# A convolution and GRU kernel: the first x chunks and cond turned by TensorE from whole rows, and three of the first chunk's four blocks convolved on 32x32 diagonal tiles

## The chip, the cores and the metric

The kernel runs on one core of one Trainium2 chip. The metric is the device time in microseconds (us) of one execution.

## The reference

The input x has 16 batch rows, 256 time steps and 512 channels, cond has 16 rows of 512 channels, all in float32. First, a causal convolution over time adds to x, channel by channel; its 16 taps are the 16 rows of cond. Then a GRU with hidden state of 512 runs over the 256 steps, starts from cond as its state, and its states are added:

```python
y = conv_general_dilated(x, cond[:, None, :], window_strides=(1,), padding=[(15, 0)],
                         feature_group_count=512)   # depthwise, causal, 16 taps
x = x + y
def cell(h, x_t):
    i_r, i_z, i_n = split(x_t @ W_ih + b_ih, 3)
    h_r, h_z, h_n = split(h @ W_hh + b_hh, 3)
    r, z = sigmoid(i_r + h_r), sigmoid(i_z + h_z)
    n = tanh(i_n + r * h_n)
    return (1 - z) * n + z * h
return x + scan(cell, cond, x)
```

## The kernel before

Channels lie on the 128 partitions, in four blocks (q = 0 to 3) along the free dimension. Partition 32 j + l of block q holds channel 128 j + 32 q + l. Time is cut into 16 chunks of 16 steps (`CHUNKS`); one block of a chunk has 16 steps x 16 batch rows = 256 columns. `xT` holds a chunk of x in this layout, with a halo of 15 steps in front, and `x1T` the convolved chunk x + conv.

The kernel writes out the order of every engine by hand: instructions run on each engine in the order in which the code issues them, and semaphores make one engine wait for another. SP's queue, ACT's queue and POOL's queue issue the transfers. The 16 steps' work of a later chunk is dealt out over the GRU's steps by `Plan`, from costs and due times; the first piece of it, `bulk.run(0, HEAD)`, is issued ahead of step 0.

What stands ahead of the GRU:

- cond (four transfers of 128 channels) and chunks 0 and 1 of x (`load_x`, L125, eight transfers each, in pieces of 512 bytes, on the SP, ACT and POOL queues) come in with 32 partitions for each j, so that a transposition of 32x32 squares by DVE gives the layout: `prepare_cond` (L192) and `turn_units` (L222).
- `load_weights` (L173) then issues W_ih and W_hh, each gate in four slices of 32 partitions, on SP and POOL. A queue reuses its semaphores in turn, so that some issues wait for the landing of an earlier transfer.
- `mark` and `idle_products(PAD)` (L350, L356) issue filler products on PE at the start; PAD is 108.
- Chunk 0 is convolved by two engines. For blocks 0 and 1, DVE does a first product with cond's last tap plus one (L554), then 15 taps each (L265), shorter and shorter. For blocks 2 and 3 (`Q_PE`), `conv_on_tensor` lets ACT make 16 diagonal matrices of 128x128 for each block (L288), and PE multiplies each by a shifted view of `xT` and adds up in PSUM (L292). ACT evicts the two results (L300).
- For chunk 1, ACT does the first products of the four blocks (`first_terms`, L239) and DVE the 15 taps of each. A tap waits for the first product of its block.
- PE then does the biases (`spread_biases`, L362), the input products of the n gate for the first 8 steps (`ni_units`, L320, evicted by ACT at L332) and those of r and z for the first two steps (`pair_units`, L383).

One GRU step (`step`) on PE is: products of r, of n, of z (L418), then some of the input products for later steps. DVE looks at r (`seen`, L398, so that DVE's wait for ACT stands there), multiplies r and h_n (L447), transposes (L449), adds (L451), transposes z (L461), and scans (L474) for the new state, which the next step's products on PE wait for. DVE's taps of the next chunk stand in the same order between the steps: in step 0, before the look at r.

Of the kernel before, what the change touches and what calls it, by code (L numbers as in the profile page):

```python
# [24 lines left out]
F32 = mybir.dt.float32  # L25
BF16 = mybir.dt.bfloat16
AF = mybir.ActivationFunctionType
ALU = mybir.AluOpType
PSUM = bass.MemoryType.PSUM

P = 128
L = 32
GT = 8
R, Z, N = 0, 1, 2
CHUNKS = (16,) * 16
PAD = 108
HEAD = 11.0
SYNC = mybir.DependencyInfo(mybir.DependencyClass.Sync, mybir.DependencyReason.DATA)
Q_PE = (2, 3)
NI = 8  # L40
AHEAD = 10
ROOM = 2.05
# [33 lines left out]
def conv_gru_kernel(  # L76
# [10 lines left out]
    nc = tc.nc  # L87
    B, T, C = x.shape
    K = cond.shape[0]
    NQ = C // P  # L90
    assert B == 16 and K == B and NQ == 4 and sum(CHUNKS) == T
    HALO = (K - 1) * B
# [5 lines left out]
    starts = [sum(CHUNKS[:c]) for c in range(NCH)]  # L98

    const = ctx.enter_context(tc.tile_pool(name="const", bufs=1))  # L100
# [5 lines left out]
    op = ctx.enter_context(tc.tile_pool(name="op", bufs=3))  # L106
    dram = ctx.enter_context(tc.tile_pool(name="dram", bufs=1, space=bass.MemoryType.DRAM))
    ps = ctx.enter_context(tc.tile_pool(name="ps", bufs=1, space=PSUM))
    ps_ni = ctx.enter_context(tc.tile_pool(name="ps_ni", bufs=2, space=PSUM))

    ctx.enter_context(tc.manual_schedule())

    def by_part(natural):
        return natural.rearrange("p (q l) -> p q l", q=NQ)
# [4 lines left out]
    def load_x(c, queues=((nc.sync,), (nc.sync,)), behind=None):  # L119

        n = CHUNKS[c]
        t = xin.tile([P, max(CHUNKS) // 2, P], F32, tag="x_nat", name=f"x_nat_{c}")
        for s in range(2):
            for j in range(NQ):
                made = queues[s][j % len(queues[s])].dma_start(  # L125
                    out=t[32 * j + B * s : 32 * j + B * s + B, 0 : n // 2],
                    in_=x[:, starts[c] + s : starts[c] + n : 2, j * P : (j + 1) * P],
                )
                if s == j == 0 and behind is not None:
                    tc.add_manual_dep(made.ins, behind.ins.name, SYNC, reason="later in time")  # L130
        x_nat[c] = t

    cond_nat = const.tile([P, P], F32)
    nc.vector.memset(cond_nat, 0.0)

    warm = const.tile([P, 1], F32)
    nc.vector.memset(warm, 0.0)
    blank = const.tile([P, 2 * P], BF16)
    nc.vector.memset(blank, 0.0)
    for j in range(NQ):  # L140
        (nc.sync, nc.scalar)[j % 2].dma_start(
            out=cond_nat[32 * j : 32 * j + B, :], in_=cond[:, j * P : (j + 1) * P]
        )
    load_x(0, ((nc.sync, nc.scalar), (nc.gpsimd,)))
    nc.scalar.activation(warm, warm, AF.Sigmoid)
    ident = const.tile([P, P], F32)
    make_identity(nc, ident)


    b_two = const.tile([2, 3 * C], F32)  # L150
# [3 lines left out]
    bn_nat = const.tile([P, P], F32)  # L154
    nc.vector.memset(bn_nat, 0.0)

    load_x(1, ((nc.sync,), (nc.gpsimd,)))
    nc.sync.dma_start(out=b_two[0:1, :], in_=b_hh.rearrange("(o c) -> o c", o=1))
    nc.sync.dma_start(
        out=b_two[1:2, 0 : 2 * C], in_=b_ih[0 : 2 * C].rearrange("(o c) -> o c", o=1)  # L160
    )
    nc.gpsimd.dma_start(
        out=bn_nat[0:P:L, :], in_=b_ih[2 * C : 3 * C].rearrange("(j c) -> j c", j=NQ)
    )


    wih_rz = const.tile([P, NQ, 2 * C], F32)
    wih_n = const.tile([P, NQ, C], F32)
    whh = [const.tile([P, NQ, C], F32, name=f"whh_{g}") for g in range(3)]

    def load_weights(w_sb, w, g, queues):
        for j in (0, 2, 1, 3):
            queues[j].dma_start(  # L173
                out=w_sb[L * j : L * j + L],
                in_=w[j * P : (j + 1) * P, g * C : g * C + w_sb.shape[2]].rearrange(
                    "(q l) c -> l q c", l=L
                ),
            )


    for tile_of, g in ((wih_n, N), (wih_rz, R)):
        load_weights(tile_of, w_ih, g, (nc.sync, nc.sync, nc.gpsimd, nc.gpsimd))
    zero_z = [const.tile([P, NQ * B * 2], F32, name=f"zero_z_{i}") for i in range(2)]
    for t in zero_z:
        nc.gpsimd.memset(t, 0.0)


    condT = const.tile([P, NQ, L], F32)
    last1 = const.tile([P, NQ], F32)

    def prepare_cond():
        nc.vector.transpose(condT, by_part(cond_nat))  # L192
        nc.vector.tensor_scalar_add(last1, condT[:, :, K - 1], 1.0)

    bnT = const.tile([P, NQ, L], F32)

# [3 lines left out]
    xT, x1T, ni = {}, {}, {}  # L200
# [3 lines left out]
    evictions = []  # L204
# [7 lines left out]
    def turn_units(c):  # L212

        def halo():
            xT[c] = xtp.tile([P, NQ, HALO + CMAX], F32, tag="xT", name=f"xT_{c}")
            if c:
                m = CHUNKS[c - 1] * B
                nc.scalar.copy(xT[c][:, :, 0:HALO], xT[c - 1][:, :, m : m + HALO])

        def turn(a):  # L220
            o = HALO + a * PAIR
            nc.vector.transpose(  # L222
                xT[c][:, :, o : o + GT * B].rearrange("p q (a r) -> p a q r", r=L),
                x_nat[c][:, a : a + GP].rearrange("p a (q l) -> p a q l", q=NQ),
            )
            if 2 * (a + GP) == CHUNKS[c] and 4 < c + 3 < NCH:
                load_x(c + 3)

        return [(0.0, halo)] + [
            (0.7, lambda a=a: turn(a)) for a in range(0, CHUNKS[c] // 2, GP)  # L230
        ]

    def first_terms(c):

        x1T[c] = x1p.tile([P, NQ, CMAX], F32, tag="x1T", name=f"x1T_{c}")
        n = CHUNKS[c] * B

        def first(q):
            nc.scalar.activation(  # L239
                x1T[c][:, q, 0:n],  # L240
                xT[c][:, q, HALO : HALO + n],
                AF.Copy,
                scale=last1[:, q : q + 1],
            )

        for q in range(NQ):
            firsts.append((c, q, lambda q=q: first(q)))

    def give_firsts(most=99):
        for _ in range(min(most, len(firsts))):  # L250
            firsts.pop(0)[2]()

    def lag(k):

        return (K - 1 - k) * B
# [19 lines left out]
            (0.135 + n / 960.0, lambda k=k, q=q: tap(k, q)) for k in range(K - 1) for q in range(NQ)  # L275
        ]

    def conv_on_tensor():

        n = CHUNKS[0] * B  # L280
        diag = const.tile([P, len(Q_PE), K, P], F32)

        def weight(k, q):
            return condT[:, q, k : k + 1] if k < K - 1 else last1[:, q : q + 1]

        for i, q in enumerate(Q_PE):
            for k in reversed(range(K)):
                nc.scalar.activation(diag[:, i, k], ident, AF.Copy, scale=weight(k, q))  # L288
        for i, q in enumerate(Q_PE):
            acc = ps_ni.tile([P, CHUNKS[0] * B], F32, tag="pni", name=f"conv_{q}")  # L290
            for k in reversed(range(K)):
                nc.tensor.matmul(  # L292
                    acc[:, lag(k) : n],
                    lhsT=diag[:, i, k],
                    rhs=xT[0][:, q, HALO : k * B + n],
                    start=(k == K - 1),
                    stop=(k == 0),
                    skip_group_check=True,
                )
            evictions.append(lambda q=q, acc=acc: nc.scalar.copy(x1T[0][:, q, 0:n], acc[:, 0:n]))  # L300


    blocks = [(t0, NI) for t0 in range(0, T, NI)]
# [43 lines left out]
    def mark():  # L347

        for i in range(2):
            nc.tensor.matmul(rz[i], lhsT=blank[:, 0:P], rhs=blank, start=True, stop=True)  # L350
            nc.tensor.matmul(nh[i], lhsT=blank[:, 0:P], rhs=blank[:, 0:P], start=True, stop=True)

    def idle_products(n):

        for _ in range(n):
            nc.tensor.matmul(  # L356
                spare[0:L, 0, 0:1], lhsT=blank[:, 0:L], rhs=blank[:, 0:1], start=True, stop=True
            )
# [180 lines left out]
    bulk = Plan()  # L539
    mark()  # L540
    idle_products(PAD)
    nc.tensor.drain()
    (_, halo), *turns = turn_units(0)
    halo()
    for t in hist:
        nc.vector.memset(t[:, 0:L], 0.0)
    prepare_cond()
    for _, fn in turns:
        fn()
    first_terms(0)  # L550
    firsts.clear()
    for q in range(NQ):
        if q not in Q_PE:
            nc.vector.tensor_scalar_mul(  # L554
# [1 line left out]
                xT[0][:, q, HALO : HALO + CHUNKS[0] * B],  # L556
                last1[:, q : q + 1],
            )
    conv_on_tensor()

    taps = [fn for i, (_, fn) in reversed(list(enumerate(tap_units(0)))) if i % NQ not in Q_PE]
    needed = (NI - 1) * (NQ - len(Q_PE))
    for fn in taps[:needed]:
        fn()
    for _, fn in turn_units(1):
        fn()
    nc.vector.transpose(bnT, by_part(bn_nat))
    for fn in taps[needed:]:
        fn()
    evictions.pop(0)()  # L570
    first_terms(1)
    give_firsts()
    evictions.pop(0)()
    spread_biases()
    nc.scalar.copy(b_rows, spare)
    seed_rz(0)
# [14 lines left out]
    for c in range(1, NCH):  # L591
        due = starts[c] - NI
        taps = tap_units(c)
# [4 lines left out]
        at = len(taps) - AHEAD  # L598
# [1 line left out]
            bulk.add(cost, due, fn)  # L600
    bulk.run(0, HEAD)

    h = (lambda kc: condT[:, kc, 0:B], condT[:, :, 0:B])
    late = []
    of_pair, of_block = [], []
    for t in range(T):
        p, s = divmod(t, 2)
# [23 lines left out]
        h = step(t, h, bulk_work, other_products)  # L631
# [41 lines left out]
```

## Time and profile before

| | |
|---|---|
| median of 3 runs | 1041.6 us (1041.51 to 1042.34) |
| profiled execution: span of the core, first to last instruction | 1039.8 us |
| distance of the span to the median | 1.8 us |
| PE busy | 1022.6 us, 98% |
| DVE busy | 926.8 us, 89% |
| ACT busy | 380.3 us, 37% |
| POOL busy | 12.4 us, 1% |
| HBM read and written | 14.73 MB and 8.39 MB |

The profiled execution has no time of its own beside its span in the page; the span leaves out what lies ahead of the first instruction and behind the last. Times in the views are us from the start of the span. In a timeline a row gives start, duration, engine, line, operation, output<-input and the count of instructions merged; in brackets stands the idle time before it and what ended it. In a table by stretch, each engine has its busy us and, in parentheses, its instructions. A matmul in float32 is recorded as two instructions. "PEld" is the loading of PE's stationary operand, which overlaps with its products.

### The profile page before, as it was taken

To read this page: it belongs to the slowest core of one execution; us is meant where nothing else is said; L and a number is where in the kernel's file an instruction comes from. 1 tells how busy PE (TensorE), PEld (TensorE's weight loads), DVE (VectorE), ACT (ScalarE), POOL (GpSimd) and SP (SyncE) were. 2 spreads that over 40 slices of the span, in tenths; PEclk is the share of its full clock that TensorE was granted. 3 is DMA by queue.
4 is the path that set the end of the run, shared out by engine and by line. 5 is a ranking of instruction groups with operands and counts; after the bars stand their busy time and mean duration, and the time that the engine had idled before them with its cause. 6 is when DMAs were issued, how large, how long until landed. Compare 5 with 4: busy or idle time off the path is not lost.

```text
span 1039.8 us, 71852 instructions
## 1 busy us (share of the span) xinstructions
PE 1022.6 (98%) x32952; PEld 928.5 (89%) x32952; DVE 926.8 (89%) x3606; ACT 380.3 (37%) x1520; POOL 12.4 (1%) x29
## 2 busy tenths in 40 slices
PE   7899999999999999999999999999999999999997
PEld 6699999999999999999999999999999999999986
DVE  7899999999999999999999999999999999896555
ACT  6233433334333333433334333343433334333332
POOL 4000000000000000000000000000000000000000
PEclk9999999999999999999999999999999999999999
DMA  9420101101010010100100010010000000000000
GB/s 216 111 58 13 26 15 29 21 15 31 8 35 14 15 35 8 32 15 19 30 14 26 14 34 15 15 34 5 15 14 15 15 13 6 15 15 15 14 11 17
DMA packets 40850, 27.72 MB, mean 27 GB/s; under 512 B 6686, under 2 KB 38498, under 8 KB 40548
## 3 DMA queue, kind: packets, MB, share of 16 engines
q1 hardware_dynamic: 38756, 18.78, 8.0%
q8 instruction: 257, 4.21, 1.7%
q0 software_dynamic: 1376, 4.20, 1.7%
q14 instruction: 45, 0.37, 0.1%
q10 hardware_dynamic: 416, 0.16, 0.1%
HBM read 14.73 MB, written 8.39 MB: 22 GB/s over the span
## 4 chain that ended last, share of the span: by engine, by line
PE 95%; DMA 3%; DVE 1%; SPq 0%; issue 0%; ACT 0%; DVEq 0%; ACTq 0%
PE prz L418 42%; PE pnh L418 21%; PE prz L383 20%; PE pni L320 10%; DMA whh<-in_L_cond_W_hh_dram 2%; DMA x_nat<-in_x_dram 1%; DVE rnT L449 0%; DVE zp L461 0%; DVE rn L447 0%; SPq L125 0%; ACT zero_z L465 0%; DVE n L451 0%; DMA out_dram<-o 0%; DVE hist L474 0%; DVE glance L398 0%
## 5 line engine op out<-in xcount | busy, mean ns | idle before, releaser
L418 PE MATMUL prz<-whh,hist 128*32 128x128 f32 x16320 | 539.9, 273 | 3.0 <-DVE hist L474 2.1
L418 PEld LDWEIGHTS prz<-whh,hist 128*32 128x32 f32 x16320 | 450.0, 103 | 8.5 <-DVE hist L474 6.6
L265 DVE SCALAR_TENSOR_TENSOR x1T<-xT,condT,x1T 128x256 f32<-128x256 f32 (+2 forms) x930 | 377.4, 462 | 0.0
L418 PE MATMUL pnh<-whh,hist 128*32 128x128 f32 x8160 | 269.7, 273 | 0.0
L383 PE MATMUL prz<-wih_rz,x1T 128*32 128x256 f32 x4096 | 268.2, 379 | 0.1
L418 PEld LDWEIGHTS pnh<-whh,hist 128*32 128x32 f32 x8160 | 226.7, 104 | 0.0
L459 ACT ACTIVATE dn<-n 128x64 f32<-128x64 f32 x256 | 67.9, 265 | 325.9 <-DVE n L451 325.9
L383 PEld LDWEIGHTS prz<-wih_rz,x1T 128*32 128x32 f32 x4096 | 129.0, 110 | 43.7 <-issue 0.3
L320 PEld LDWEIGHTS pni<-x1T,wih_n 128*32 128x32 f32 x4096 | 122.8, 110 | 42.7 <-ACT x1T L300 0.6
L435 ACT ACTIVATE r<-prz 128x128 f32<-128x128 f32 x256 | 71.1, 278 | 238.6 <-PE prz L418 235.5
L320 PE MATMUL pni<-x1T,wih_n 128*32 128x128 f32 x4096 | 158.1, 273 | 0.0
L474 DVE TENSOR_TENSOR_SCAN hist<-zero_z,dn 128x32 f32<-128x32 f32 (+1 forms) x768 | 128.6, 216 | 0.0
L447 DVE TENSOR_TENSOR rn<-r,pnh 128x128 f32<-128x128 f32 x256 | 72.4, 283 | 38.5 <-PE pnh L418 37.2
L465 ACT ACTIVATE zero_z<-zp 128x32 f32<-128x32 f32 x512 | 90.6, 226 | 8.6 <-DVE zp L461 1.8
L449 DVE STREAM_TRANSPOSE rnT<-rn 128x128 f32<-128x128 f32 x256 | 79.7, 311 | 8.7
L461 DVE STREAM_TRANSPOSE zp<-prz 128x128 f32<-128x128 f32 x256 | 80.9, 316 | 1.8 <-PE prz L418 1.7
L332 ACT ACTIVATE ni<-pni,bnT 128x128 f32<-128x128 f32 x128 | 47.1, 368 | 74.7 <-PE pni L320 74.7
L467 DVE TENSOR_TENSOR dn<-hist,dn 128x64 f32<-128x64 f32 x255 | 58.4, 229 | 11.3
L451 DVE TENSOR_TENSOR n<-rnT,ni 128x64 f32<-128x64 f32 x256 | 57.7, 225 | 8.9
L398 DVE COPY glance<-r 1x1 f32<-1x1 f32 x256 | 34.0, 133 | 25.3 <-ACT r L435 25.3
L371 ACT COPY prz<-b_rows 128x256 f32<-128x256 f32 x128 | 48.5, 379 | 0.0
L398 DVE COPY glance<-zero_z 1x1 f32<-1x1 f32 x256 | 36.3, 142 | 8.0 <-ACT zero_z L465 0.3
(51 smaller groups left out, 211.1 us busy)
## 6 DMA issues: line engine op xcount, KB each, us to landing
out_dram<-o SPq DMA_DIRECT2D x248, 32.0 KB, 1.7
x_nat<-in_x_dram SPq DMA_DIRECT2D x118, 64.0 KB, 3.0
whh<-in_L_cond_W_hh_dram POOLq DMA_DIRECT2D x8, 256.0 KB, 14.7
wih_rz<-in_L_cond_W_ih_dram POOLq DMA_DIRECT2D x2, 512.0 KB, 10.2
wih_rz<-in_L_cond_W_ih_dram SPq DMA_DIRECT2D x2, 512.0 KB, 14.3
whh<-in_L_cond_W_hh_dram SPq DMA_DIRECT2D x4, 256.0 KB, 19.0
x_nat<-in_x_dram POOLq DMA_DIRECT2D x8, 64.0 KB, 5.4
wih_n<-in_L_cond_W_ih_dram POOLq DMA_DIRECT2D x2, 256.0 KB, 7.7
```

The source lines that it names most:

```text
L265: nc.vector.scalar_tensor_tensor(out=x1T[c][:, q, to], in0=xT[c][:, q, k * B + to.start : k * B + n], scalar=condT[:, q, k : k + 1], in1=x ...
L320: nc.tensor.matmul(hold[q][32 * j : 32 * j + 32, 0:n], lhsT=wih_n[:, kc, j * P + q * L : j * P + q * L + L], rhs=x1T[c][:, kc, o : o + n], ...
L383: nc.tensor.matmul(rz[p % 2][32 * j : 32 * j + 32], lhsT=x1T[c][:, kc, o : o + PAIR], rhs=w_rz[:, :, j * P : (j + 1) * P], start=False, st ...
L398: nc.vector.tensor_copy(glances[i][0:1], of_scalar[0:1, 0:1])
L418: product = nc.tensor.matmul(dst[32 * j : 32 * j + m], lhsT=h[0](kc), rhs=whh[g][:, kc, j * P : (j + 1) * P], start=False, stop=(kc == NQ ...
L435: of_r = nc.scalar.activation(r, pr, AF.Sigmoid)
L447: nc.vector.tensor_mul(rn, r, pnh)
L449: nc.vector.transpose(rnT, by_part(rn))
L459: nc.scalar.activation(dn_v[:, :, :, 1], n, AF.Tanh)
L461: nc.vector.transpose(zp, by_part(pz))
L465: nc.scalar.activation(z_v[:, qs, :, 1], zp[:, qs, half], AF.Sigmoid) for qs in halves
L474: nc.vector.tensor_tensor_scan(hist_g[:, lo + at : lo + end], z[:, to], dn[:, to], 0.0, op0=ALU.mult, op1=ALU.add,)
```

## The change

`load_rows` replaces `load_x` for chunks 0 and 1: four transfers of 128 whole rows of x (half a chunk each, 2 KB a row), two on SP's queue and two on ACT's, none on POOL's. cond comes as one transfer of 16 rows on ACT's queue. `turn_by_tensor` multiplies 32-column slices of these rows by the identity on PE, 16 products for each tile, into one PSUM buffer (`turning`); DVE copies cond and chunk 0 out of it, ACT copies chunk 1.

`Q_PE` gets block 1 too, so DVE keeps block 0 alone. A diagonal matrix is no longer 128x128: `make_diag` makes for each block the four 32x32 diagonals of all 16 taps in one tile, with one product over 15 taps and one for the last (block 1 on DVE, blocks 2 and 3 on POOL, none on ACT). `conv_on_tensor` issues four products for each tap, each on 32 rows and 32 columns of PE, into one accumulator. Between the three convolutions PE turns the two halves of chunk 1. W_ih's issues now stand behind the diagonals in POOL's order, and so does the transfer of b_ih's n part. PAD is 72 and the drain behind the filler products is gone. The evictions of the three convolutions on ACT, all three, now stand ahead of chunk 1's first products.

```diff
-PAD = 108
+PAD = 72
-Q_PE = (2, 3)
+Q_PE = (1, 2, 3)
...
+    turning = ctx.enter_context(tc.tile_pool(name="turning", bufs=1, space=PSUM))
...
-    cond_nat = const.tile([P, P], F32)
-    nc.vector.memset(cond_nat, 0.0)
+    def load_rows(c, half, queue):
+        t = const.tile([P, C], F32, name=f"x_rows_{c}_{half}")
+        t0 = starts[c] + half * GT
+        queue.dma_start(out=t, in_=x[:, t0 : t0 + GT, :].rearrange("b t c -> t b c"))
+        x_rows[c, half] = t
+    x_rows = {}
+    cond_nat = const.tile([B, C], F32)
...
-    for j in range(NQ):
-        (nc.sync, nc.scalar)[j % 2].dma_start(
-            out=cond_nat[32 * j : 32 * j + B, :], in_=cond[:, j * P : (j + 1) * P]
-        )
-    load_x(0, ((nc.sync, nc.scalar), (nc.gpsimd,)))
+    nc.scalar.dma_start(out=cond_nat, in_=cond)
+    for c in range(2):
+        for half in range(2):
+            load_rows(c, half, (nc.sync, nc.scalar)[half])
...
+    ident_l = const.tile([P, L], F32)
+    nc.vector.tensor_reduce(out=ident_l, in_=ident.rearrange("p (i l) -> p l i", l=L),
+                            op=ALU.add, axis=mybir.AxisListType.X)
...
-    load_x(1, ((nc.sync,), (nc.gpsimd,)))
...
+    def turn_by_tensor(turned, rows, unit):
+        for q in range(NQ):
+            for j in range(NQ):
+                at = j * P + q * L
+                nc.tensor.matmul(turned[L * j : L * j + L, q], lhsT=rows[:, at : at + L],
+                                 rhs=unit, start=q == 0, stop=q == NQ - 1,
+                                 skip_group_check=True)
     def prepare_cond():
-        nc.vector.transpose(condT, by_part(cond_nat))
+        turned = turning.tile([P, NQ, K], F32, tag="turned", name="cond_turned")
+        turn_by_tensor(turned, cond_nat, ident[0:B, 0:B])
+        nc.vector.tensor_copy(condT, turned)
         nc.vector.tensor_scalar_add(last1, condT[:, :, K - 1], 1.0)
+    def turn_rows(c, half, engine):
+        turned = turning.tile([P, NQ, P], F32, tag="turned", name=f"x_turned_{c}_{half}")
+        turn_by_tensor(turned, x_rows[c, half], ident)
+        to = xT[c][:, :, HALO + half * P : HALO + half * P + P]
+        ...  # copied by ACT or by DVE
...
+    def make_diag(engine, q):
+        diag[q] = const.tile([P, K, L], F32, name=f"diag_{q}")
+        parts = ((slice(0, K - 1), condT[:, q, 0 : K - 1]), (slice(K - 1, K), last1[:, q : q + 1]))
+        for to, w in parts:
+            n = to.stop - to.start
+            engine.tensor_tensor(out=diag[q][:, to], op=ALU.mult,
+                in0=ident_l.unsqueeze(1).broadcast_to([P, n, L]),
+                in1=w.unsqueeze(2).broadcast_to([P, n, L]))
...
-        for i, q in enumerate(Q_PE):
-            for k in reversed(range(K)):
-                nc.scalar.activation(diag[:, i, k], ident, AF.Copy, scale=weight(k, q))
...
-                nc.tensor.matmul(acc[:, lag(k) : n], lhsT=diag[:, i, k],
-                    rhs=xT[0][:, q, HALO : k * B + n], ...
+            for j in range(NQ):
+                rows = slice(L * j, L * j + L)
+                nc.tensor.matmul(acc[rows, lag(k) : n], lhsT=diag[q][rows, k],
+                    rhs=xT[0][rows, q, HALO : k * B + n], ...
...
-    nc.tensor.drain()
...
     prepare_cond()
-    for _, fn in turns:
-        fn()
+    make_diag(nc.vector, Q_PE[0])
+    for q in Q_PE[1:]:
+        make_diag(nc.gpsimd, q)
+    nc.gpsimd.dma_start(out=bn_nat[0:P:L, :], ...)
+    for tile_of, g in ((wih_n, N), (wih_rz, R)):
+        load_weights(tile_of, w_ih, g, (nc.sync, nc.sync, nc.gpsimd, nc.gpsimd))
+    turn_units(0)[0][1]()
+    turn_rows(0, 0, nc.vector)
+    turn_rows(0, 1, nc.vector)
     first_terms(0)
...
-    conv_on_tensor()
+    conv_on_tensor(Q_PE[0])
+    turn_units(1)[0][1]()
+    turn_rows(1, 0, nc.scalar)
+    for q in Q_PE[1:]:
+        if len(evictions) > 1:
+            evictions.pop(0)()
+        conv_on_tensor(q)
+        if q == Q_PE[1]:
+            turn_rows(1, 1, nc.scalar)
...
-    for fn in taps[:needed]:
-        fn()
-    for _, fn in turn_units(1):
+    for fn in taps:
         fn()
     nc.vector.transpose(bnT, by_part(bn_nat))
-    for fn in taps[needed:]:
-        fn()
-    evictions.pop(0)()
     first_terms(1)
+    while evictions:
+        evictions.pop(0)()
     give_firsts()
-    evictions.pop(0)()
     spread_biases()
```

## The prediction

> **What bounds the kernel now.** The page's chain that ended last came first: PE holds 95% of the span, DMA 3%. The table by stretch shows PE full from 40 us on. A change that touches only what stands before step 0 therefore moves the end by as much as it moves the moment from which PE never stops.
>
> ```profile
> PE 95%; DMA 3%; DVE 1%; SPq 0%; issue 0%; ACT 0%; DVEq 0%; ACTq 0%
> ```
> ```profile
> 20.00:25.00 5.00, 5.00 (x142) 4.03 (x141) 5.00 (x14) 2.77 (x8) 0.55 (x1) 1.00 1.03 268
> ...
> 40.00:50.00 10.00, 10.00 (x344) 8.96 (x336) 9.66 (x38) 4.16 (x16) 0.00 (x0) 1.00 0.30 83
> ```
>
> (After the stretch: its length, then busy us of PE, PEld, DVE, ACT, POOL, the clock, the share of the DMA engines, GB/s.) The chain in order of time names that moment. The last W_hh slice lands at 34.07, its z products run, and from 36.33 PE goes on without a gap. I call 36.33 the restart.
>
> ```profile
> 11.42 22.65 DMA whh<-in_L_cond_W_hh_dram
> 34.07 0.14 issue
> 34.20 1.10 PE prz L418 x32
> ...
> 36.33 1.08 PE prz L418 x32
> ```
>
> So the start is bound by DMA, whose engines are full (share 1.03). The timeline of DVE shows how little lies behind that:
>
> ```profile
> 15.94 15.99 DVE L265 SCALAR_TENSOR_TENSOR x1T<-xT,condT,x1T 128x128 f32<-128x128 f32 x48
> 31.85 0.13 DVE L398 COPY glance<-r 1x1 f32<-1x1 f32 x1
> 32.78 0.29 DVE L447 TENSOR_TENSOR rn<-r,pnh 128x128 f32<-128x128 f32 x1 [0.80 <-PE pnh L418]
> ```
>
> The last 32 of these 48 are chunk 1's taps (28 of the head start, 4 of step 0); they start at 19.18, 0.396 us apart: 12.67 us. Step 0's look at r stands behind them in DVE's order. In step 1 PE starts again 1.85 us after that look (38.46 to 40.31, nothing else late). By DVE alone the restart would be 31.85 + 1.85 = 33.7: DVE has 2.6 us to spare, and what delays chunk 1's taps by more costs all beyond that.
>
> **What releases chunk 1's taps.** A tap needs ACT's first term of its block. In ACT's order before, the first terms follow the *first* convolution's eviction:
>
> ```profile
> 16.14 0.37 ACT L300 COPY x1T<-conv 128x256 f32<-128x256 f32 x1 [1.51 <-PE conv L292]
> 16.41 1.71 ACT L239 ACTIVATE x1T<-xT,last 128x256 f32<-128x256 f32 x4
> ```
>
> After, they follow all three evictions, because the loop that empties the list stands ahead of them. So chunk 1's taps wait for the end of the *third* convolution on PE. The rest is a sum of when that is.
>
> **Prices on PE.** Two rows of the products on 128x128 tiles, the same shapes (256 down to 176 columns) twice, show the clock, although the clock column says 1.00 for both:
>
> ```profile
> 9.36:13.52 4.16, 4.15 (x11) 3.76 (x12) 1.00 1.03 210
> 15.95:17.92 1.97, 1.97 (x12) 1.89 (x12) 1.00 1.03 292
> ```
>
> 4.16 us against 1.97: until 13.5 PE ran at half speed, after 4.2 us of unbroken products at full. The filler products (1.96 to 5.00) had not raised it. An f32 product is two instructions; on four column tiles, at full speed, 16 instructions of 256 columns take 0.86 us and 32 of 128 take 0.87, so 0.21 ns per column and instruction, four tiles at a time. No row shows four row tiles at once; the nearest are these.
>
> - A convolution after: 16 taps of 256 down to 16 columns (2,176 in all), each on four diagonal tiles: 2,176 x 4 x 2 x 0.21 = 3.7 us. The other end: nothing under 128 columns is cheaper than 128 (the filler's starts lie 26.7 ns apart however small): 4.4 us. I take 3.7, since the starts to four tiles lie 7 ns apart in the trace. At half speed 7.4.
> - Turning half a chunk of x: 16 products of 128 columns, 32 instructions: 0.87 us, at half speed 1.7.
> - The convolutions of before took 11.2 us for two blocks; three now take 11.1, one after another.
>
> On the four diagonal tiles the Trainium skill speaks against the change: "TensorEngine Tiling (Array Packing)", section Restrictions and Gotchas, says that different row tiles cannot access one PSUM bank at a time, and all four write one `acc`. Four times 3.7 would be 14.8 us a block and a time near 1080. But here each row tile writes partitions of its own, and the page does not say that the chip would wait, so I leave it to a rival.
>
> **The sum, in us from the start.**
> 1. The memset of cond_nat goes, so PE starts at 1.1; 72 fillers at 26.7 ns end at 3.75. cond is one transfer on ACT's queue, issued near 1.03; the 8 KB ones took 1.6 to 1.8 to land, so it is there. 16 small products at half speed, 0.5 to 0.9: take 0.7, and 0.2 to drain: 4.65. DVE's copy (64 columns, rows of 0.18 to 0.23): 4.9.
> 2. x, first half: its buffer is cond's, so PE starts at 4.95. The rows (issued at 1.0 to 1.9, 2 KB packets where 512 B were) should land by 4.5 to 5.5; 64 KB in 512 B pieces took 4.9. 1.7 at half speed and a drain: 6.85. DVE meanwhile makes block 1's diagonals (480 columns at the taps' 1.04 ns and 0.13: 0.63, plus 0.16 for last). Copy of 512 columns by the same: 0.66, 7.5. Second half, one buffer, so after that copy: 7.55 to 9.45; copy 10.1. Before, both transposes were through at 9.2.
> 3. First convolution: 3.5 us at half speed until 13.6 does 1.75 of its 3.7; the rest ends at 15.5.
> 4. x of chunk 1, first half, behind it in PE's order: 16.4. Second convolution: 20.1. Second half: 21.0. The third convolution's accumulator is the first's, and ACT evicts that only after both its copies of x: drain 0.2, copy 0.6 (rows: 384 columns 0.48, 960 columns 0.98), eviction 0.35: PE stands 1.1, to 22.1. Third convolution: 25.8.
> 5. Eviction and first term (0.37 and 0.43, starts 0.27 apart, drain and signals): 26.7. Taps: +12.67 = 39.4. Restart +1.85: 41.2, against 36.33: 4.9 later.
>
> Beside these, priced at nothing: DVE's single block of chunk 0 (a first product 0.3, 16 sizes at half of the 7.9 that two blocks took, 3.9) ends near 14.5, under PE's convolutions. On POOL the eight x issues (4.2 us) go; ahead of bn_nat and its W_ih and W_hh issues now stand four diagonal products that wait for last1 at 5.1. A 128-column select took 0.29; 480 columns cost 0.29 to 1.08 each: take 1.1 and 0.3 twice, so POOL issues from about 7.9 where bn_nat went at 6.13. The second convolution wants these diagonals at 16.4. bn_nat took 5.8 to land: 14, and DVE is idle then. SP loses eight issues (6 of them 2.78 us), so its weights, behind b_two's memset (near 3.6), start by 4.3 rather than 6.89. The bytes are the same, x's packets are four times fewer; W_hh should land between 29 and 36. A landing costs landing + 2.26 (34.07 to 36.33), so it decides only past 39. PE's biases (0.8), head products (3.85 and 1.2 of waits for ACT), pair (1.9) and step 0 (4.0) run from 25.8 to 37.6; zp is wanted at 39.4 + 0.9. DVE is last, alone.
>
> The sum goes on the median: 1041.6 + 4.9 = 1046.5. The page gives the profiled execution's span, 1039.8, 1.8 below the median; I keep that distance, so the span should be near 1044.7.
>
> **The rivals.**
> - *The clock rises early.* If filler, cond and x products (1.1 to 9.4 with two gaps under 1 us) raise it by about 6.8, the second half of x is 0.85 cheaper and the first convolution 1.75: restart 38.6, time 1043.9. For it: PE is busier there than before. Against: the filler did not raise it before. "TensorE: Matmul & The Clock Gate", Part 1, says that about 3.4 us of sustained activity is needed in a window that does not start with the kernel, so the phase decides; by the page alone either case could come.
> - *Short products at the 26.7 ns floor:* three times 0.7, 1048.6 with the late clock, 1046.0 with the early one.
> - *Row tiles one after another:* 3 x 11.1 more, near 1080.
> - *Faster: the queue's relief decides.* W_hh then lands near 30, and the restart falls to DVE. This needs the taps to start by 21.8 (36.33 - 1.85 - 12.67); with the early clock a convolution would have to cost 2.9 us. If they started at 19.2 as now, the restart would be 33.7 and the time 1039.0. Against it: 2.9 is a fifth under the column price that every four-tile row shows.
>
> **How the numbers follow.** 0.2%, about 2.1 us, is what a measurement here can tell from no change. Late clock, with either product price: 0.50 (1046.5 to 1048.6). Early clock: 0.36 (1043.0 to 1046.0, its lower end if x and cond are also half a us sooner); 0.15 of that lies under 1043.7. Serial tiles or another cost above 1052: 0.07. Faster: 0.07. The range 1042.8 to 1052 leaves out about 0.17. Faster 0.07, same 0.15, slower 0.78.
>
> **What would show it.** Right: in the timeline of DVE a hole of about 12 us between chunk 0's last tap and chunk 1's first, ended by ACT's first terms, which follow the eviction of the third convolution; glance of r near 39; W_hh landed before its products; convolutions of 3.7 us at full speed. Wrong: a first chunk 1 tap before 21.8; convolutions under 3 us or over 5; W_hh still last in the chain; a gap on PE after the restart.

## The result, and the profile after

The changed kernel takes 1059.5 us (median of 4 runs, 1058.2 to 1060.3), the kernel before beside it 1042.0: 1.016 times as long, 95% interval 1.014 to 1.018. The direction was right, and 1059.5 lies above the range (1042.8 to 1052.0). The profiled execution took 1059.2 us, with a span of 1057.4 where 1044.7 was forecast: 12.7 us too little.

The page's chain still belongs to PE; DVE's share is now 3% (1% before) and that of "issue" 1% (0% before):

```profile
PE 96%; DVE 3%; issue 1%; ACT 0%; DVEq 0%
```

The chain in order of time (start, us, what, and how many instructions of it) shows where the time lies. The restart is now 52.58 (36.33 before, 41.2 forecast):

```profile
17.71 1.14 PE conv L336 x17
18.85 2.12 issue
20.98 4.76 PE conv L336 x95
25.73 0.66 PE x_turned L206 x17
26.40 2.45 issue
28.85 1.11 PE x_turned L206 x15
...
30.99 6.22 PE conv L336 x126
...
38.05 12.77 DVE x1T L301 x32
...
52.58 1.93 PE prz L462 x32
54.51 1.69 PE pnh L462 x32
```

Three things are to be seen. Twice PE stops in the middle of a loop of products, for 2.12 and 2.45 us, with nothing that it waits for ("issue"); both times 17 instructions into a new tile. The third convolution takes 6.22 us, where 3.7 was priced. And after the restart 32 instructions of r take 1.93 and those of n 1.69, where such a group at full speed takes 0.87.

The timeline of DVE has the hole that was forecast, but 21 us of it and not 12. It is ended by ACT's first term, and then come the 32 taps and the look at r:

```profile
38.05 12.77 DVE L301 SCALAR_TENSOR_TENSOR x1T<-xT,condT,x1T 128x256 f32<-128x256 f32 x32 [21.07 <-ACT x1T L275]
50.73 0.14 DVE L442 COPY glance<-r 1x1 f32<-1x1 f32 x1
```

The table by stretch (after the stretch: length, busy us of PE, PEld, DVE, ACT, POOL, the clock, the share of the DMA engines, GB/s), cut where the clock changes, explains the slow products:

```profile
21.90:25.30 3.40, 3.40 (x75) 3.32 (x69) 0.00 (x0) 0.00 (x0) 0.83 (x2) 0.50 1.07 289
25.30:28.70 3.40, 1.10 (x49) 0.80 (x42) 0.00 (x0) 0.00 (x0) 0.55 (x1) 1.00 1.03 242
28.70:35.50 6.80, 5.59 (x67) 3.42 (x71) 0.00 (x0) 1.14 (x3) 0.00 (x0) 0.50 0.85 187
...
52.60:56.00 3.40, 3.40 (x66) 3.35 (x70) 2.32 (x8) 0.45 (x2) 0.00 (x0) 0.51 0.02 5
```

All edges of the clock lie on a grid of 3.41 us (15.09, 21.92, 25.33, 28.74, 35.57, 52.64, 56.05). The first stop lies in 18.5 to 21.9, the second in 25.3 to 28.7, the wait for the taps in 49.2 to 52.6: each time the next stretch runs at half speed. DMA is full (1.03 to 1.07) around both stops.

### The profile page after: what moved, and what is told of

Its sections match the earlier page's. It is cut to its first block, busy times and chain, and to the rows that moved or that the text cites. A ratio compares the mean times of both kernels' runs of the same rounds, so it can differ in the third digit from the quotient of the medians.

```text
span 1057.4 us, 72669 instructions
## 1 busy us (share of the span) xinstructions
PE 1036.2 (98%) x33396; PEld 933.9 (88%) x33396; DVE 924.5 (87%) x3590; ACT 372.7 (35%) x1491; POOL 11.0 (1%) x25
## 4 chain that ended last, share of the span: by engine, by line
PE 96%; DVE 3%; issue 1%; ACT 0%; DVEq 0%
PE prz L462 42%; PE pnh L462 21%; PE prz L427 20%; PE pni L364 10%; PE conv L336 2%; DVE x1T L301 1%; PE x_turned L206 1%; DVE rnT L493 0%; DVE rn L491 0%; DVE zp L505 0%; ACT zero_z L509 0%; DVE n L495 0%; PE spare L400 0%; DVE hist L518 0%; DVE xT L229 0%
## 5 line engine op out<-in xcount | busy, mean ns | idle before, releaser
L301 DVE SCALAR_TENSOR_TENSOR x1T<-xT,condT,x1T 128x256 f32<-128x256 f32 (+1 forms) x915 | 374.6, 464 | 21.6 <-ACT x1T L275 21.1
L427 PEld LDWEIGHTS prz<-wih_rz,x1T 128*32 128x32 f32 x4096 | 126.4, 110 | 45.1
```

Of the source, the lines that this page charges most:

```text
L301: nc.vector.scalar_tensor_tensor(out=x1T[c][:, q, to], in0=xT[c][:, q, k * B + to.start : k * B + n], scalar=condT[:, q, k : k + 1], in1=x ...
L427: nc.tensor.matmul(rz[p % 2][32 * j : 32 * j + 32], lhsT=x1T[c][:, kc, o : o + PAIR], rhs=w_rz[:, :, j * P : (j + 1) * P], start=False, st ...
```

## The theories

*Instruction fetch.* Between the weights' packets the trace has single packets of a queue that carries PE's instructions, 16,384 bytes each. The whole run has 261 of them for PE's 33,396 recorded matmuls, and the kernel before 257 for 32,952: one for every 128. The convolution on small tiles issues 128 of them per block where the 128x128 diagonals issue 32, and does so while the DMA engines are full. If the next packet comes late, PE stands at the end of what it has, and the stop lowers the clock for the next 3.4 us or more. Here is the table of the DMA queues between 18 and 21 us (packets, MB, share of 16 engines): the one packet ended at 19.34 (packet times are from the trace's own records), and PE went on at 20.98.

```profile
q0 software_dynamic: 139, 0.50, 67.2%
q1 hardware_dynamic: 110, 0.24, 32.0%
q8 instruction: 1, 0.02, 2.5%
```

The trace of before has one such stop, which the prediction passed over, because W_hh landed later anyway. In PE's timeline of before:

```profile
29.46 0.95 PE L418 MATMUL prz<-whh,condT 128*16 128x128 f32 x27 [1.14 <-issue]
```

It comes at PE's 346th recorded matmul, the first stop after the change at its 349th.

*Rivals.* The row tiles wait for one another in PSUM; PE waits for x or the diagonals; or the price of the change is its many small products alone, whatever the transfers do. The runs with fewer bytes (e2, e12) and with shifted counts (e5) part them from the first.

## The experiments

Times are medians, each with its ratio to the kernel before on the same chip and the 95% interval; numbers of matmuls are counts in PE's record from its first. Edits are against the changed kernel unless "before" is named.

**e2_no_weight_transfers: no weights in the way.**

```diff
-        for j in (0, 2, 1, 3):
-            queues[j].dma_start(out=w_sb[L * j : L * j + L], in_=w[...])
+        nc.gpsimd.memset(w_sb, 0.001)
```

> The changed kernel without the transfers of W_ih and W_hh: POOL fills the weights with a constant instead, so their values are left out and the DMA engines are nearly idle from 8 us on. Theory (fetch): the two stops of PE of 2.1 and 2.5 us inside the second convolution and the second turning are fetches of PE's instructions (16 KB, 128 products' worth) that queue behind the weight transfers; without these transfers there is no stop over 0.5 us, the clock stays up after it has risen, the third convolution ends at 26 to 28.5 and the restart is near 42 to 44: 1047 to 1051. Rival (tiles): the stops belong to products on four row tiles, to their accumulator or to the change of tile shape: they stay at 2 us and more, and the time is within 3 us of 1059.5.

1049.7 us, 1.007 (1.006 to 1.009). The chain has neither stop, and the convolutions at full speed take what was priced:

```profile
17.97 3.86 PE conv L330 x127
...
23.92 3.99 PE conv L330 x125
...
28.74 12.77 DVE x1T L295 x32
...
43.28 1.93 PE prz L456 x32
45.21 1.43 PE pnh L456 x32
```

From first start to last start, the 128 instructions of the second and third take 3.76 and 3.75 us. So the row tiles do run beside one another, in one accumulator, and neither the small products nor x explain the 12.7 us. The weights' transfers cost 9.8 us; what is left over the forecast is 3.2. The packets of instructions show it too: the second starts at 13.73 here and at 18.12 in the changed kernel, although PE is equally far at 15.0 (the 221st matmul starts at 15.01 and at 14.89). It comes 4.4 us later, when the weights are in the way.

**e5_fewer_fillers: shift the count.** If stops come by count, 32 fillers fewer move them to 32 instructions later in the convolutions; if they come from data or time, they stay where they were.

```diff
-PAD = 72
+PAD = 40
```

> The changed kernel with 40 filler products instead of 72, so that every later product stands 32 earlier in PE's stream. Theory (fetch): PE stops at the same places counted in products from the start, behind products 349 and 477 (every 128), that is 49 product instructions into the second convolution instead of 17, and 49 later in place again for the second stop, at the 17th product of the third convolution's 128, no longer in the turning of x. Rival (tiles): the stops stay with the same products, 17 into the second convolution and 17 into the turning. Time within 2 us of 1059.5 by both.

1058.1 us in one run. The chain:

```profile
15.69 1.14 issue
...
18.65 2.44 PE conv L336 x49
21.09 3.49 issue
...
29.84 1.04 PE conv L336 x16
30.88 2.23 issue
```

The stop that came 17 instructions into the second convolution comes 49 into it, and the one that came in the middle of x's turning comes 16 into the third convolution; x is turned without a break. Counted from PE's first matmul they stand at the 349th and 476th (in the changed kernel at the 349th and 477th), and a third at the 222nd. (The changed kernel passes that one: its first packet started at 6.10, e5's at 13.86.) They are 127 or 128 apart: the count decides, not what the product is.

**e1_first_terms_early: ACT's order.** Chunk 1's first products before the evictions.

```diff
     first_terms(1)
+    give_firsts()
     while evictions:
         evictions.pop(0)()
-    give_firsts()
```

> The changed kernel with one order changed: on ACT, chunk 1's four first products stand ahead of the evictions of the second and third convolution (and behind that of the first, as PE needs). Theory (the order passes on every delay of the third convolution): chunk 1's taps start about 31 us, right behind ACT's copy of chunk 1's second half (30.6), not at 38.05, and end near 44; then PE is last, its z products of step 0 end at 47 to 48, so the restart is 48.2 to 49.3 instead of 52.6; with PE idle for about 1 us there instead of 4.4, step 1 runs at full speed, 1.8 less. Time 1053 to 1055. Rival (the taps wait for something else than that order): no change, 1058 to 1060.

1054.5 us, 1.012 (1.009 to 1.014), so 5 us less. The first tap comes at 31.36 instead of 38.05 and the last ends at 44.11, but the restart is at 51.23, where 48.2 to 49.3 was expected (the profiled execution took 1056.2, 1.7 above the median): now PE is last. It stops a third time, for 2.52 us at the 604th matmul, inside the third convolution, and its last z products before the restart end at 50.2. The gate that the prediction named is real, and with it gone the stops still hold the start.

**e3_rows_and_turning_alone and e4_convolutions_alone: the halves of the change.** e3 has the rows, the turning on PE and PAD, and keeps two blocks on 128x128 diagonals, made by ACT. e4 keeps x as before and has the three blocks on small tiles, with ACT's order of e1.

```diff
 # e3
-Q_PE = (1, 2, 3)
+Q_PE = (2, 3)
...
+    diag = const.tile([P, len(Q_PE), K, P], F32)
...
+                nc.scalar.activation(diag[:, i, k], ident, AF.Copy, scale=weight(k, q))
 # e4, against before
-Q_PE = (2, 3)
+Q_PE = (1, 2, 3)
...
+    make_diag(nc.vector, Q_PE[0])
+    for q in Q_PE[1:]:
+        make_diag(nc.gpsimd, q)
```

> One part of the change alone: x and cond by whole rows and turned by PE; the convolution stays as before (blocks 2 and 3 on 128x128 diagonals made by ACT, two blocks on DVE), PE turns chunk 1 around the first convolution, DVE copies its first half, ACT its second. Without diagonals on POOL its weight issues start near 1.6 us. Both theories: few products, no stop of note; chunk 1's taps from 20 to 21.5, PE's z products of step 0 end at 34 to 36, W_hh landed by 30 to 32, restart 35 to 37.5: 1040 to 1043, within 0.2% of before. If the turning itself were the cost of the change, the time would be over 1050.

1043.4 us, 1.001 (1.000 to 1.002): the rows bring nothing and cost next to nothing. Taps start at 19.95, and the last weights land at 35.55 (30 to 32 was expected). One stop of 2.36 us, among step 0's r products, is mostly covered by that landing: z's products, which need these weights, start at 36.38.

> The other part alone: x and cond come and are transposed by DVE as before; three blocks convolved on 32x32 diagonal tiles, diagonals on DVE and POOL, chunk 1's first products ahead of the second and third eviction. DVE then has an early end of its taps (near 30). Theory (fetch): three blocks of 128 product instructions meet full DMA engines, PE stops for 2 to 3.5 us twice, the third convolution ends at 28 to 30, restart 40 to 42.5: 1045 to 1048.5. Rival (the clock and the wait for x alone, no stops): the third convolution ends near 24, restart 36.3 to 37.3: 1041.5 to 1043.

1050.6 us, 1.008 (1.006 to 1.009), above what either theory gave. The taps of chunk 1 are through at 31.15 and the restart is at 46.95, so PE is last: it stops for 3.29 and 2.02 us, and runs at half speed from 22.5 to 29.3 and from 32.7 to 39.5. Half speed costs at least as much here as the stops themselves: PE is busy for 12.6 us of these two stretches, half of which (6.3, an estimate) full speed would save, and the stops are 5.3. Of the two halves, the convolutions carry the loss; but the halves together (0.8 and 8.0 us over the kernel before) are less than the change's 17.5. The change's order on ACT, which neither half has, is 5.0 of the rest (e1); some 3.7 is seen in no part alone.

**e11_two_blocks_small_tiles: the tiles alone.** e4 with the two blocks of before. Against the kernel before, the size of the tiles and who makes them differ, and what e4 brings with it: W_ih's issues stand behind the diagonals on POOL, and ACT's order is e1's.

```diff
 # against e4
-Q_PE = (1, 2, 3)
+Q_PE = (2, 3)
```

> The kernel before with only the tiles changed: blocks 2 and 3 on 32x32 diagonals (made by DVE and POOL), blocks 0 and 1 on DVE, x and cond as before. Theory (fetch): 256 product instructions instead of 64 meet full DMA engines: stops of 2 to 4 us at product 346 and 474 from the start, second convolution ends at 22.5 to 24.5, restart 38 to 41: 1043.5 to 1047. Rival (tiles at their own price, 3.8 us a block, no stops): the convolutions end near 19.5, restart 36.3, within 0.8 of before.

1046.9 us, 1.004 (1.002 to 1.005). PE does the same sums with four times the instructions, and is later for it: stops of 3.06 us at the 351st and 2.59 at the 477th matmul, half speed from 22.4 to 29.2 and from 32.6 to 36.0, restart at 41.99 (36.33 before). The last weight packet ends at 35.68 (33.63 before), so part of the delay could be the later weights; the chain from 9.82 to 40.10 is PE's work and stops alone.

**e7_three_blocks_big_diagonals: fewer instructions for the same blocks.** The changed kernel with 128x128 diagonals: 32 instructions a block instead of 128, each on the whole array.

```diff
...
-            for j in range(NQ):
-                rows = slice(L * j, L * j + L)
...
-                    acc[rows, lag(k) : n], lhsT=diag[q][rows, k], rhs=xT[0][rows, q, ...]
+                    acc[:, lag(k) : n], lhsT=diag[:, i, k], rhs=xT[0][:, q, ...]
```

> The changed kernel with the same three blocks on PE in the same order, but on 128x128 diagonals made by ACT: 32 product instructions for a block instead of 128, with a longer time for each block (4.4 us and more, and paced by ACT's diagonals until 19). Theory (fetch): 288 instructions fewer before step 0, so no stop within the convolutions; third convolution ends at 28 to 29.5, first tap of chunk 1 at 29 to 30.5, restart 43.5 to 45: 1048.5 to 1052, so the slower convolutions win 8 us and more. Rival (three blocks and the order alone make the loss, the count of instructions does not matter): 1058 to 1063.

1052.1 us, 1.009 (1.008 to 1.011), at the upper edge of what was expected and 7.4 less than with small tiles. No stop; the second and third convolution take 4.59 and 4.68 us, 0.7 longer than the small tiles in e2, and yet the first tap comes at 30.60 instead of 38.05. POOL makes no diagonals here, so its weights are issued from 3.82 instead of 8.27 and the last packet ends at 34.68 instead of 37.19; but the DMA engines were as full while the convolutions ran (share 1.04 to 1.05 from 18 to 30). The small products that are cheaper on PE are dearer here, since they empty PE's instructions four times as fast.

**e9_before_third_of_weights and e12_after_third_of_weights: a third of the bytes.** Both load the r and z parts of W_ih alone, two of six gates; the other weights are views of that tile.

```diff
...
-    whh = [const.tile([P, NQ, C], F32, name=f"whh_{g}") for g in range(3)]
+    wih_n = wih_rz[:, :, 0:C]
+    whh = [wih_rz[:, :, 0:C], wih_rz[:, :, C : 2 * C], wih_rz[:, :, 0:C]]
...
-    for tile_of, g in ((wih_n, N), (wih_rz, R)):
+    for tile_of, g in ((wih_rz, R),):
...
-    for g in (R, N, Z):
...
-        load_weights(whh[g], w_hh, g, (nc.sync, second, nc.gpsimd, nc.gpsimd))
```

> The kernel before with only the r and z columns of W_ih transferred and read in place of all weights (2.1 MB instead of 6.3; the other weights' values are left out), and nothing added on POOL, whose constant fills held a DVE instruction for 8 us in the run without weight transfers. It tests again that the start of the kernel before is bound by the landing of W_hh, with DVE 2.6 us behind: restart 33.5 to 34.5 instead of 36.3, 1039 to 1040.5. If PE or DVE bound it already: 1041.5 and more.

1040.1 us, 0.997 (0.996 to 0.998). With W_hh out of the way the kernel before is bound by DVE's taps:

```profile
16.26 15.91 DVE x1T L265 x48
...
33.95 1.08 PE prz L418 x32
```

The prediction gave 33.7 for a restart by DVE alone.

> The changed kernel with a third of the weights' bytes, in the same way as for the kernel before and with nothing added on POOL. Theory (fetch): weights are through near 16 us, no stop of PE over 1 us behind that, third convolution ends at 27 to 29, first tap of chunk 1 at 28 to 30, restart 42.5 to 45: 1047.5 to 1051. Rival: the stops stay, 1058 and more.

1052.3 us (1050.8 to 1054.4), 1.009 (1.007 to 1.011); above what was expected, and 7.2 less than with all the weights. The last weight packet ends at 22.25 instead of 37.19. One stop is left, the one before that moment, and it is followed by 3.4 us at half speed. The stop at the 477th matmul is gone, and the third convolution is at full speed:

```profile
17.99 1.81 issue
19.80 4.77 PE conv L336 x98
...
26.65 3.99 PE conv L336 x125
```

The wait before the restart is followed by half speed until 50.95, 6.8 us in all (3.4 in the changed kernel). That and the one stop are what lies above the forecast. So, in one and the same kernel, the stop comes while weights arrive and not after.

**e8_before_no_weight_transfers: the same for before; inconclusive.** Edit as in e2.

> The kernel before without the transfers of W_ih and W_hh (POOL fills the weights with a constant, their values are left out). It tests the reading that the start of the kernel before is bound by the landing of W_hh, with DVE 2.6 us behind: restart 33.5 to 34.2 instead of 36.3, time 1039 to 1040. If PE or DVE bound it already, 1041.5 and more.

1048.7 us, 1.006 (1.005 to 1.008), a miss. The memsets that stand in for the weights ran on POOL from 6.75 to 17.55, and in DVE's timeline the first two products of chunk 0, 0.3 us each otherwise, were held for as long:

```profile
9.92 8.04 DVE L548 TENSOR_SCALAR x1T<-xT,last 128x256 f32<-128x256 f32 x2
```

All taps of chunk 1 came 8 us late (27.26). e2 has the same stall (8.25 us), but there DVE waits for PE's convolutions afterwards anyway, until 28.74. e9 answered what e8 was for.

**e6_fillers_before_restart and e10_wide_fillers_before_restart: hold the clock.** Between PE's last products before the restart (48.2) and the restart (52.6) PE does nothing, and the next 3.4 us run at half speed. Both fill that wait with products that nothing uses: e6 with 140 of one column, e10 with 68 of 128 columns.

```diff
+        if t == 0:
+            idle_products(140)                      # e6
+            for _ in range(68):                     # e10
+                nc.tensor.matmul(spare[0:L, 0], lhsT=blank[:, 0:L], rhs=blank[:, 0:P],
+                                 start=True, stop=True)
```

> The changed kernel with 140 filler products behind step 0's z products, where PE waits 4.4 us for DVE. Theory (the clock falls in that wait): fillers hold it from 48.2 to 52, and step 1's r and n products take 0.87 us each instead of 1.9 and 1.7: 1.8 less, 1057 to 1058.3; the restart stays at 52 to 53. If the half speed after the restart has another cause, no change, 1059.5 within 0.6.

1058.5 us, 1.016 (1.015 to 1.018), between the two forecasts. The clock tells more: PE was busy with fillers from 46.7 to 50.3, and still ran at half speed from 50.1 to 53.6.

```profile
46.70:50.10 3.40, 3.40 (x145) 3.40 (x137) 3.33 (x12) 0.00 (x0) 0.00 (x0) 1.00 0.02 5
50.20:53.50 3.30, 2.62 (x53) 2.42 (x54) 3.00 (x12) 0.97 (x5) 0.00 (x0) 0.50 0.02 5
```

> The changed kernel with 68 filler products of 128 columns behind step 0's z products (3.7 us), where 140 fillers of one column (the same time) did not keep the clock up. Theory (the clock's gate counts columns that stream, not instructions): full speed in step 1, 1.8 less, 1057 to 1058.3. Rival (it wants something else, such as products that differ or f32): half speed as before, 1059.5 within 0.8.

1059.4 us, 1.016 (1.014 to 1.018): no gain in the median. But the clock held, as the table by stretch and the chain show:

```profile
49.50:53.80 4.30, 4.00 (x78) 3.82 (x68) 4.10 (x16) 0.61 (x3) 0.00 (x0) 1.00 0.01 4
53.80:56.00 2.20, 2.12 (x80) 2.12 (x84) 2.20 (x8) 0.45 (x2) 0.00 (x0) 1.00 0.00 0
```
```profile
53.88 1.08 PE prz L462 x32
54.96 0.87 PE pnh L462 x32
```

From the restart to the end of the span there are 1003.1 us (1057.0 - 53.9), against 1004.8 in the changed kernel and 1004.3 in e6, so 1.7 us are saved. They are lost again ahead of it: in this execution the stops took 3.50 and 2.01 us (2.12 and 2.45 in the profiled execution of the changed kernel, 1.54 and 4.00 in e6's), although the three kernels are the same up to there. The stops vary by more than the effect that the median was to show.

## Why the prediction was wrong

- *Mechanism.* Right: ACT's order, the wait of the taps for the third convolution, the 12.7 us of taps (12.77) and the 1.85 from the look at r to the restart (1.76 from the last tap's end). e1 shows that the order costs what it should, and e9 that the kernel before had 2.4 us between DVE's and W_hh's restart (36.33 - 33.95), where 2.6 was given.
- *Prices on PE.* 3.7 us for a convolution at full speed was right (3.75 in e2). The Trainium skill, "TensorEngine Tiling (Array Packing)", Restrictions and Gotchas, states that different row tiles cannot access a PSUM bank at the same time; in e2 four of them wrote separate partitions of one accumulator, and a block took 3.75 us, not four times that.
- *The step that failed* is the sum's steps 3 and 4, which let PE's stream run without a stop from 10.1 to 22.1 and at full speed from 13.6 on. To the first tap the sum gave 26.7; it was 38.05. Of these 11.35 us, the start of the second convolution (17.64 instead of 16.4) is 1.2; the second convolution, 8.1 instead of 3.7, is 4.4 (the stop, and half speed after it); x's turning, 4.2 instead of 0.9, is 3.3 (the second stop); the third convolution at half speed is 2.5; what is left over, -0.1. So two stops and the clock that follows them are 10.2 of the 11.35.
- *The restart at half speed* was not in the sum either: PE stands for 4.4 us while DVE finishes, and pays 1.3 us after it (1004.8 from restart to end, 1003.5 before). With the 11.4 by which the restart is late, that is the 12.7.
- *The rivals.* The early clock did not come (recorded full from 15.1), nor the floor, nor the waiting row tiles, nor taps before 21.8. Stops on PE were in none of them.
- *The clock at the start.* The sum had 13.6 for it; with the first convolution's start at 10.57 for 10.1 this is the 1.2 above. In e2 the clock rose at 15.5, in e12 at 13.4: it moves with the grid.
- *DVE's single block* took 5.8 us where 3.9 was put, and ended at 16.7, still under PE's convolutions: it cost nothing.
- *W_hh* landed at 37.2 instead of 29 to 36; POOL's queue, issued to from 8.27, delivered its first bytes at 14.1. It was not last, as forecast. The relief by fewer packets did not show: the rows of x took until 12.4 beside the weights.
- *What could have been read.* The stop at 28.33 in the trace of before and its "issue" were in the views, and so were nine packets of instructions within the first 60 us; I priced the change's instructions by PE's time and not by their number. "Runtime: NRT & Kernel Launch", section Instruction fetch mechanics, states that an engine's instructions come in 16 KiB blocks over a DMA queue, the next while the current one runs, and that the crossing is mostly hidden. The size agrees with these traces (16,384 bytes), and so does the lead (in e2, with no weights in the way, the first four packets landed about 70 to 130 matmuls ahead of their use). That it is hidden holds here where the DMA engines are not full (e2, and e12 after 22 us) or where a packet's 128 matmuls last longer (e7).

Shown are that the stops come by the count of matmuls (e5), need weights in flight (e2, e12) and go when a block has a quarter of the instructions (e7). The packets close the case: there are 19 such stops in ten of the traces (the kernel before with one, the changed kernel, e1, e3, e4, e5, e6, e10, e11 and e12), and in every one PE goes on 1.33 to 1.76 us after the end of a packet of instructions. Where the packet waits in those 4 us, whether for its queue's turn or behind bytes under way, no record shows, and it was not tried.

No version of the change beat the kernel before; e3 equals it, and the one thing that helped the kernel before, fewer bytes ahead of the restart (e9), is not in this change.

## What to carry to other kernels

Count instructions as well as time: a loop of many short products that runs while large loads fill the DMA engines can use up its instructions faster than they arrive, and each stop costs its own 1.1 to 4.0 us and, in most cases, half the clock for 3.4 us or more (14 of the 19 stops; the other five, of 1.14 to 2.52 us, left the clock full). Where the start of a kernel is full of transfers, take the form with fewer and longer instructions, even if PE's busy time is greater (e7: 0.7 us more per block than the small tiles undisturbed, and 7.4 less in all than the changed kernel). Before moving work from one engine to another, look at which order on a third engine then releases the next stage.

## What the runs showed of the hardware

- A packet with PE's instructions (16,384 bytes, for 128 recorded matmuls) came 4.4 us later with weights in flight than without, and PE stopped for 1.1 to 3.5 us, in one execution 4.0.
- A stop of 1.81 us was followed by half the clock (e12), while one of 2.52 us (e1) and one of 2.23 us (e5), each lying across an edge of the 3.41 us grid, were not.
- 140 one-column fillers that kept PE busy for 3.5 us did not hold the clock (0.50 afterwards, e6); 68 of 128 columns did (1.00, e10). Each is one execution.
- A row of memsets on POOL held DVE's float32 product with a scalar for some 8 us, in e2 and in e8 (two products took 8.04 us in e8; 0.62 before, and in e9, which has no such memsets). DVE's transposes of 32x32 squares, 1.30 us for two at 8.58 in e8, under the same memsets, took as long as before.
- Whole rows of 2 KB over two queues: 1.05 MB of x came in 6.8 us with no weights beside them (2.25 to 9.06 in e2), some 154 GB/s; beside the weights the last row came at 12.4.
